# Attention block in fp32r and fp16: two of the four fp32 copies of the attention output are made by POOL instead of ScalarE

## The chip, the cores and the metric

The kernel runs on one core of one Trainium2 chip. The metric is the device time of one execution in microseconds (us); the time of a kernel is the median over its runs. Five engines work side by side and are kept in step by semaphores: PE (TensorE: matmuls, with PEld for its weight loads), DVE (VectorE), ACT (ScalarE), POOL (GpSimd) and SP (SyncE, which here only issues DMAs). Each engine runs its own instructions in the order in which they were written.

## The reference

A group norm with 32 groups over x (4 batches, 512 channels, 48 x 48 = 2304 tokens) is followed by self attention with 8 heads of 64 channels and by an output projection, and x is added:

```
hn  = group_norm(x) * scale + bias
qkv = (qkv_w @ hn + qkv_b)  as fp16           # (b, 3, 8 heads, 64, 2304)
w   = softmax((q*s)^T (k*s))                  # s = 64 ** -0.25
a   = (w @ v)  as fp32                        # (b, 512, 2304)
out = x + proj_w @ a + proj_b
```

## The kernel before

The work is cut into four batches, four pairs of heads in each batch (a pair is 128 channels, so it fills the partitions; g counts the 16 pairs, g = 4b + pair), and for each pair five blocks of queries: four of 512 tokens and a last one of 256 (`QBLOCKS`, j = 0 to 4).

The main loop walks over `stream`, a list of units. A unit is one sixth of a 512-block (one third of a 256-block): three bursts, each with two or four score matmuls on PE (L949) into one of three PSUM tiles `ps`, and one exponential on ACT (L956) from that tile to a fp16 tile `p`. Two units later PE multiplies those exponentials with v (L974). DVE adds up the exponentials for the softmax sums (L1003, tile `acc`; both inputs are in SBUF), at the end of a block with two further adds (L1006).

When a block of a pair is complete, DVE copies the product from PSUM (L983, `avx`), PE sums `acc` over the partitions (L1026), DVE copies the sums (L1042), and DMAs on SP's queue bring them to a small tile and, inverted, back as rows (`sums`, `row`, `ib`). POOL then checks the sums (L1064 and L1065, four small instructions per block, in `check_sums`) and makes `att`, the fp16 attention output: `att = avx * ib` (L1090, in `divide`). POOL also computes `rstd` of the group norm (L631). That is nearly all of what POOL does in the main loop.

The output projection of batch b runs beside the attention of the first pair of batch b+1 (for the last batch, in the last pair and the tail). For each block j, `att32` copies the block of `att` of all four pairs to fp32 tiles `a` (tags `a32_0` to `a32_3`, one buffer each), with ACT at L832. `proj_chain` then runs over the pairs c = 0 to 3 and multiplies each copy with a high and a low part of the weights (L838, eight matmuls in one PSUM bank for one chunk of 128 output channels); there are four chunks per block. DVE adds the bias and the residual (L865) and frees the one bank `pw`, and SP stores the result.

Because the tiles `a` have one buffer, the copies of block j+1 wait until PE has read those of block j for the last time, which is in the last chunk of block j: pair c = 2 is read for the last time by its sixth matmul, pair c = 3 by its eighth.

Where each piece of work goes is decided when the program is written out: `beside` is a hand-ordered list of the pieces of projections, `put_convert` puts the copies of a block (through `begin` in `proj_pieces`) between the chunks of block j and those of block j+1, and `fill` takes pieces from the list after each unit as a credit in microseconds allows. In ACT's order the copies of a block therefore stand between two units' exponentials, in POOL's order between the checks and divisions of whatever blocks are under way.

In the last batch the blocks j = 2, 3, 4 are handled in two parts: `FIRST` (pairs 0 to 2, three copies) and `LAST` (pair 3 alone, one copy). Of the 80 copies, 16 have 256 columns and 64 have 512.

Of the kernel before, what the change touches and what calls it, by code (L numbers as in the profile page):

```python
# [27 lines left out]
NC = C // P  # L28
NPAIR = HEADS // 2
# [438 lines left out]
def fast_path(  # L468
# [12 lines left out]
    nc = tc.nc  # L481
# [303 lines left out]
    atts, res, at32 = {}, {}, {}  # L785
# [32 lines left out]
    def left_over(b, j):  # L818

        return b == B - 1 and j >= NQ - 2  # L820

    def att32(b, j, pairs=range(NC)):
        o, n = QBLOCKS[j]
        for c in pairs:
            if left_over(b, j):
                t = xpool.tile([P, n], F32R, tag=f"x{c}_{j}", name=f"a32_{b}_{j}_{c}")
            else:
                t = work.tile(
                    [P, QB], F32R, tag=f"a32_{c}", bufs=1, name=f"a32_{b}_{j}_{c}"
                )  # L830
            at32[b, j, c] = t[:, :n]
            nc.scalar.copy(at32[b, j, c], atts[b * NPAIR + c][:, o : o + n])  # L832

    def proj_chain(b, j, m, ps, pairs=range(NC)):
        n = QBLOCKS[j][1]
# [52 lines left out]
    def proj_pieces(b, j):  # L888

        def ahead(k):
            if k < len(proj_list) and not in_two(b, proj_list[k][0]):
                residual(b, *proj_list[k])

        def begin():
            att32(b, j, LAST if in_two(b, j) else range(NC))
            if j == 0:
                ahead(0)
                ahead(1)  # L900

        pairs = LAST if in_two(b, j) else range(NC)
        chains = [
            proj_piece(b, j, chunks, pairs, lambda k=k: ahead(k + 2))
            for k, (jj, chunks) in enumerate(proj_list)
            if jj == j
        ]
        return [piece(0.0, begin)], chains
# [271 lines left out]
    for b in range(B):  # L1180
# [20 lines left out]
        if b == B - 1:  # L1201
            put_qk(g + 3, 1)
            put_qk(g + 3, 0, range(NQ - 1))
            put_convert(old, 0)
            put_qk(g + 3, 0, (NQ - 1,))

            ahead = [
                (residual, b, j, chunks)
                for j in (NQ - 2, NQ - 3, NQ - 1)
                for jj, chunks in proj_list  # L1210
                if jj == j
            ]
            for j in range(NQ):
                put_proj(old, j, ahead)
                if j + 1 < NQ:
                    put_convert(old, j + 1)

            for j in (NQ - 2, NQ - 3, NQ - 1):
                there = ends[(NG - 2) * NQ + j] + BEHIND + 6
                put_run(att32, b, j, FIRST, after=there)  # L1220
                put_first(b, j)
            put_convert(b, 0)
            put_proj(b, 0)
            put_convert(b, 1)
            put_proj(b, 1)
            put_convert(b, NQ - 3)
            put_proj(b, NQ - 3)
            continue
# [120 lines left out]
    for n in range(end):  # L1349
# [25 lines left out]
        if n - BEHIND in soon:  # L1375
            g, j = stream[n - BEHIND][:2]
# [9 lines left out]
    g, b, j = NG - 1, B - 1, NQ - 1  # L1386
    n = QBLOCKS[j][1]
    values(stream[-2])
    while loads:
        loads.popleft()[1]()  # L1390
    check_sums(g, NQ - 2)
    att32(b, NQ - 2, LAST)

    def last_banks(name):
# [21 lines left out]
    o = QBLOCKS[j][0]  # L1416
# [39 lines left out]
@with_exitstack  # L1456
def group_norm_attention(ctx: ExitStack, tc: tile.TileContext, *args):
    nc = tc.nc
    keep = ctx.enter_context(tc.tile_pool(name="keep", bufs=1))
    flag = keep.tile([1, 1], I32, name="flag")  # L1460

    kinds = mybir.EngineType
    engines = {kinds.PE, kinds.DVE, kinds.Pool, kinds.SP, kinds.Activation}
    with tc.manual_schedule(engines=engines):
        fast_path(tc, flag, *args)
    fails = nc.values_load(
        flag[0:1, 0:1],
        min_val=0,
        max_val=1,
        skip_runtime_bounds_check_because="it is the result of a comparison",  # L1470
    )
    with tc.If(fails > 0, label="fallback"):
        general_path(tc, *args)
# [37 lines left out]
```

## Time and profile before

| what | value |
|---|---|
| median of 3 runs | 1616.85 us (1616.51 to 1617.53) |
| profiled execution, its own time | 1617.42 us |
| its span (first to last instruction) | 1615.6 us |
| granted TensorE clock | 0.998 |
| ACT copies L832 | 80, 40.7 us, mean 596 ns |
| POOL multiplications L1090 | 78, 117.7 us, mean 1508 ns |
| DVE adds L1003 | 270 of 1796 ns and 79 of 1748 ns (means) |
| ACT idle, waiting for PE's scores | 298.4 us |
| PE idle, waiting for ACT's exponentials | 5.3 us in 12 waits |

The first lines of the page give each engine's busy time, its share of the span and its number of instructions. The groups of instructions give, for one line of the kernel, the engine, what it writes and reads, how often, its busy time and the mean of one. The list of waits says which engine sat idle until which other engine or DMA had finished: total, number, longest. In the timeline a row has the start, the duration, the engine, the line and, in square brackets, the idle time just before it with what ended it.

### The profile page before, as it was taken

How to read it: one execution, taken by the hardware profiler on the slowest of the kernel's cores; microseconds unless marked ns; L12 is line 12 of the kernel's file. 1: busy time of each engine (PE TensorE's matmuls, PEld its weight loads, DVE VectorE, ACT ScalarE, POOL GpSimd, SP SyncE). 2: the span in 40 equal slices, each digit the busy share in tenths (PEclk: the TensorE clock that was granted, in tenths of full speed). 3: DMA queues.
4: the chain of work that ended last, by engine and by line, in shares of the span. 5: the costliest groups of instructions: out<-in, count | busy, mean ns of one | idle time of the engine just before them, and what ended most of it. 6: DMA issues, size and time to landing. Idle time of an engine off the chain costs nothing. (4 is left out here: it accounts for less than half of the span.)

```text
span 1615.6 us, 28324 instructions
## 1 busy us (share of the span) xinstructions
PE 1583.1 (98%) x11500; PEld 695.5 (43%) x11500; DVE 1135.7 (70%) x1301; ACT 1283.0 (79%) x1398; POOL 293.8 (18%) x421
## 2 busy tenths in 40 slices
PE   7999999999999999999999999999999999999996
PEld 2533434443333534555333353455533334434544
DVE  6267668866666668986666666898667666667775
ACT  3077777888888888888887888887888888888894
POOL 1001112212121211212111121121211121211212
PEclk9999999999999999999999999999999999999999
DMA  7002020000000023511000002352100000016424
GB/s 217 6 14 67 11 66 22 18 14 11 14 18 14 13 65 119 158 50 28 14 11 18 14 12 60 98 162 72 31 14 12 14 18 15 15 24 188 123 61 132
DMA packets 94897, 82.11 MB, mean 51 GB/s; under 512 B 50852, under 2 KB 60964, under 8 KB 94756
## 3 DMA queue, kind: packets, MB, share of 16 engines
q1 hardware_dynamic: 92724, 78.35, 17.8%
q8 instruction: 92, 1.51, 0.4%
q10 hardware_dynamic: 1904, 1.84, 0.4%
q14 instruction: 49, 0.40, 0.1%
q0 software_dynamic: 128, 0.01, 0.0%
HBM read 60.70 MB, written 19.17 MB: 49 GB/s over the span
## 5 line engine op out<-in xcount | busy, mean ns | idle before, releaser
L956 ACT ACTIVATE p<-ps 128x1024 f16<-128x1024 f32 x1296 | 1231.9, 1027 | 298.9 <-PE ps L949 298.4
L1003 DVE TENSOR_TENSOR acc<-acc,p 128x3072 f16<-128x3072 f16 x270 | 485.0, 1796 | 77.0 <-ACT p L956 76.2
L709 PE MATMUL pqk<-x,wqkv 128*64 128x512 f32 (+1 forms) x2464 | 519.3, 551 | 0.0
L949 PE MATMUL ps<-q,k 64*128 64x512 f16 (+1 forms) x2880 | 359.5, 358 | 6.3 <-ACT p L956 5.3
L974 PE MATMUL av<-p,v 128*64 128x512 f16 (+1 forms) x2880 | 361.1, 364 | 0.4 <-DVE slx L1042 0.3
L760 PE MATMUL pv<-wqkv,x 128*64 128x256 f32 x2304 | 268.6, 380 | 0.0
L709 PEld LDWEIGHTS pqk<-x,wqkv 128*64 128x64 f32 x2464 | 168.9, 137 | 224.2 <-issue 166.8
L1064 POOL TENSOR_SCALAR in<-sums 128x8 f32<-128x8 f32 (+1 forms) x158 | 112.5, 712 | 782.3 <-DMA sums<-slx 775.9
L949 PEld LDWEIGHTS <-k 64*128 64x128 f16 x2880 | 107.4, 94 | 286.1 <-issue 238.3
L974 PEld LDWEIGHTS <-v 128*64 128x64 f16 x2880 | 131.9, 109 | 211.3 <-issue 167.1
L1090 POOL TENSOR_TENSOR att<-avx,ib 128x512 f16<-128x512 f32 (+1 forms) x78 | 117.7, 1508 | 468.7 <-DMA ib<-row 398.5
L760 PEld LDWEIGHTS pv<-wqkv,x 128*64 128x64 f32 x2304 | 160.1, 137 | 92.8 <-issue 4.5
L1003 DVE TENSOR_TENSOR acc<-p,p 128x3072 f16<-128x3072 f16 x79 | 138.1, 1748 | 0.0
L838 PE MATMUL pr<-a,whi 128*128 128x512 f32 (+1 forms) x311 | 121.8, 399 | 1.7 <-DVE q L719 1.1
L838 PE MATMUL pr<-a,wlo 128*128 128x512 f32 (+1 forms) x311 | 113.5, 372 | 0.0
L1006 DVE TENSOR_TENSOR acc<-acc 128x1024 f16<-128x1024 f16 x156 | 109.2, 700 | 5.3
L719 DVE TENSOR_SCALAR q<-pqk,bqkv 128x512 f16<-128x512 f32 (+1 forms) x79 | 54.9, 695 | 80.3 <-PE pqk L709 79.8
L719 DVE TENSOR_SCALAR k<-pqk,bqkv 128x512 f16<-128x512 f32 (+1 forms) x75 | 52.1, 695 | 77.9 <-PE pqk L709 77.8
L768 DVE TENSOR_TENSOR v<-pv,bv 128x512 f16<-128x512 f32 x72 | 49.7, 691 | 80.5 <-PE pv L760 80.2
L983 DVE COPY avx<-av 128x512 f32<-128x512 f32 (+1 forms) x79 | 50.6, 640 | 66.1 <-PE av L974 66.1
L865 DVE SCALAR_TENSOR_TENSOR r<-pr,bproj,r 128x512 f32<-128x512 f32 (+1 forms) x80 | 54.9, 694 | 43.2 <-PE pr L838 42.6
L838 PEld LDWEIGHTS pr<-a,whi 128*128 128x128 f32 x311 | 58.4, 188 | 38.6 <-issue 18.5
(68 smaller groups left out, 451.0 us busy)
## 6 DMA issues: line engine op xcount, KB each, us to landing
r<-x_dram SPq DMA_DIRECT2D x72, 256.0 KB, 3.2
out_dram<-r SPq DMA_DIRECT2D x69, 256.0 KB, 2.1
ib<-row SPq DMA_DIRECT2D x126, 128.0 KB, 3.1
x<-x_dram SPq DMA_DIRECT2D x62, 256.0 KB, 4.2
x<-x_dram SPq DMA_DIRECT2D x16, 128.0 KB, 4.9
sums<-slx SPq DMA_DIRECT2D x128, 2.0 KB, 2.1
ib<-row SPq DMA_DIRECT2D x30, 64.0 KB, 3.2
wqkv<-qkv_wT_dram SPq DMA_DIRECT2D x2, 768.0 KB, 6.9
```

Source lines behind the costliest of these rows:

```text
L709: nc.tensor.matmul(pw[0][lo : lo + D, :n], wqkv[:, c, w0 + lo : w0 + lo + D], hn[b, c, j], start=(c == 0), stop=(c == NC - 1),)
L719: nc.vector.tensor_scalar(qk[g][part][:, o : o + n], pw[0][:, :n], bqkv[:, col : col + 1], SCALE, ALU.add, ALU.mult,)
L760: nc.tensor.matmul(pw[0][lo : lo + D, a, :], hn[b, c, i * P // QB][:, at + lo : at + lo + D], wqkv[:, c, 2 * C + half * C // 2 :][:, : C / ...
L838: nc.tensor.matmul(ps[:, :n], w[:, c, bass.ts(m, P)], at32[b, j, c], start=(i == 0), stop=(i == len(steps) - 1),)
L865: nc.vector.scalar_tensor_tensor(xt[:, i], places[i], bias, xt[:, i], ALU.add, ALU.add)
L949: nc.tensor.matmul(ps[:, h, a * n : (a + 1) * n], kt[rows, bass.ts(i, P)], qt[rows, o : o + n], start=True, stop=True,)
L956: nc.scalar.activation(pt[:, r], ps, AF.Exp)
L974: nc.tensor.matmul(av[0][lo : lo + D, :n], vv[b, pr // 2][:, i, pr % 2 * P + lo : pr % 2 * P + lo + D], pt[:, r, h, a * n : (a + 1) * n], ...
L1003: nc.vector.tensor_tensor(t, before, pt, ALU.add)
L1006: nc.vector.tensor_tensor(t[:, 0], t[:, 0], t[:, r], ALU.add)
L1064: nc.gpsimd.tensor_scalar(t, sm, limit, None, op)
L1090: nc.gpsimd.tensor_tensor(atts[g][:, o : o + n], avx.pop((g, j))[:, :n], ibs.pop((g, j))[:, :n], ALU.mult,)
```

## The change

`att32` makes the copies of the third and fourth pair (c = 2 and 3) with POOL instead of ACT, wherever it is called for more than one pair. The calls for one pair (`LAST`) are as before, and so are the buffers, PE's, DVE's and SP's instructions and their order.

```
+    beside_exps = range(NC // 2, NC)
+
     def att32(b, j, pairs=range(NC)):
...
             at32[b, j, c] = t[:, :n]
-            nc.scalar.copy(at32[b, j, c], atts[b * NPAIR + c][:, o : o + n])
+            source = atts[b * NPAIR + c][:, o : o + n]
+            if c in beside_exps and len(pairs) > 1:
+                nc.gpsimd.tensor_copy(at32[b, j, c], source)
+            else:
+                nc.scalar.copy(at32[b, j, c], source)
```

## The prediction

> **What bounds the kernel now.** I read the page's first line, then the list of waits, then PE's timeline around every cast at L832. The first line says that PE is the bound:
>
> ```profile
> PE 1583.1 (98%) x11500; PEld 695.5 (43%) x11500; DVE 1135.7 (70%) x1301; ACT 1283.0 (79%) x1398; POOL 293.8 (18%) x421
> ```
>
> PE is idle for 32.5 us of the span, mostly at both ends. So ACT's time is worth nothing in itself; it counts only where its lateness reaches PE. The waits say how often:
>
> ```profile
> ACT p L956 <- PE ps L949: 298.4, 391, 46.7
> ...
> PE ps L949 <- ACT p L956: 5.3, 12, 0.5
> ```
>
> ACT waits 298.4 us for PE, PE only 5.3 us for ACT. But those 5.3 us sit where the change works. Of PE's 12 waits for exponentials, ten follow a block's casts by 4 to 5 us: at 630.22 (0.52), 667.19 (0.39), 1038.46 and 1039.37 (0.16 + 0.52), 1077.14 (0.38), 1092.37 (0.39), 1456.16 (0.52), 1492.54 (0.38), 1542.85 (0.52), 1563.55 us (0.52). Sum: 4.30 us. There are stalls too short for a row of their own: six score matmuls take 0.82 us in 351 of PE's groups, but 0.95 to 1.13 us in seven groups after the other casts (651.38, 681.43, 1061.61, 1507.14, 1528.79, 1555.24, 1578.22). The excess over 0.82 is 1.36 us. The casts cost PE **5.66 us** in all.
>
> [...] POOL's small L1065 has a median of 205 ns and a maximum of 1804, about L1003's 1750; L1003 itself reaches 2851 beside an L1090. Whoever waits gets in after the one running operation: at 1030.14 and 1030.93 us POOL's checks run 0.70 and 0.60 us, one DVE add each.
> [...] I therefore use starts and what waits for them.
>
> **What is moved.** Fifteen blocks of batches 0 to 2 and two of batch 3 move two casts each, three blocks of batch 3 one each: 37, of which 7 have 256 columns. None issues a DMA; PE's, DVE's and SP's orders stay. Durations:
>
> ```profile
> L1090 POOL TENSOR_TENSOR att<-avx,ib 128x512 f16<-128x512 f32 (+1 forms) x78 | 117.7, 1508 | 468.7 <-DMA ib<-row 398.5 <-DVE acc L1003 47.6 <-ACT p L956 11.4
> ...
> L832 ACT CAST a<-att 128x512 fp32r<-128x512 f16 (+1 forms) x80 | 40.7, 596 | 2.7 <-POOL att L1053 2.3 <-PE pr L838 0.5
> ...
> L1430 POOL TENSOR_SCALAR fines<-inv 128x256 f32<-128x256 f32 x1 | 0.9, 853 | 0.1
> ...
> L1434 POOL COPY fines<-fine 128x8 f32<-128x8 f32 x1 | 0.2, 187 | 0.0
> ```
>
> *ACT.* Four casts take 2.19 us, so a further one costs (2.19 - 0.64)/3 = 0.52 us (0.31 with 256 columns). ACT loses 30 x 0.52 + 7 x 0.31 = 17.8 us, 1.04 us per full block. Each stall above is 0.13 to 0.68 us, and no more than what its block gives up. So all **5.66 us** can go, except the 0.68 at 1038 to 1039 us: there the first projection waits 1.10 us for DVE at 1044.88, and DVE for a sums DMA at 1043.09, which a faster ACT does not bring earlier. **Gain 4.98 us.**
>
> *One POOL copy, d.* The trace has none of this size. Below: the 187 ns of the 8-column copy plus 504 columns at the 0.84 ns of POOL's memsets (128x96 217 ns, 128x8 143) is 0.61 us. Above: at the 2.51 ns per column of POOL's tensor_scalar (256 columns 853 ns, 8 columns 231) it is 1.45 us. [...] I take **0.85 us**[...].
>
> *When the copies can start, and when they are needed.* A copy waits for the last read of the old tile. In blocks 1 to 4 that is in the last chunk of the block before, at about the moment ACT's casts start now. PE's next chain begins 1.4 to 2 us later and reads pair 2 1.03 us and pair 3 1.49 us after that. So POOL has 2.5 to 3.4 us for 2 x 0.85 = 1.70 us, if it is free and has the port. In six blocks the release is long past or other chains come first, and nothing can be late: block 0 of each batch, and block 4 of batches 0 and 1. The three `FIRST` copies go early too. I went through the rest with POOL's and DVE's timelines. Blocks 1 of all batches, block 2 of batch 0 and blocks 3 and 4 of batch 2 fit, with DVE adds pushed by up to 0.7 us into idle time. Four do not:
>
> (1) Batch 1, block 2. POOL has L1090 and L631 ahead of the copies, and then DVE holds the port:
>
> ```profile
> 1070.89 1.77 POOL L1090 TENSOR_TENSOR att<-avx,ib 128x512 f16<-128x512 f32 x1 [5.91 <-DMA ib<-row]
> ...
> 1072.15 2.19 ACT L832 CAST a<-att 128x512 fp32r<-128x512 f16 x4
> ...
> 1072.77 0.72 POOL L631 TENSOR_TENSOR rstd<-veps,mhalf 128x2 f32<-128x2 f32 x1
> ...
> 1073.35 1.74 DVE L1003 TENSOR_TENSOR acc<-acc,p 128x3072 f16<-128x3072 f16 x1
> ...
> 1075.12 0.40 PE L838 MATMUL pr<-a,whi 128*128 128x512 f32 x1
> 1075.13 1.42 DVE L1006 TENSOR_TENSOR acc<-acc 128x1024 f16<-128x1024 f16 x2
> ...
> 1077.14 0.39 PE L949 MATMUL ps<-q,k 64*128 64x512 f16 x2 [0.38 <-ACT p L956]
> ```
>
> The first copy can be issued at 1073.55, behind L1003's start, gets the port at 1075.1 and is ready at 1076.05[...]; the row at 1075.12 wants it: 0.93 late. The second waits for the first L1006 (to 1076.55), is ready at 1077.5 and wanted at 1076.51: 1.0. **1.9 us.**
>
> (2) Batch 2, block 2. L1090 stands ahead and waits for its DMA:
>
> ```profile
> 1487.55 2.19 ACT L832 CAST a<-att 128x512 fp32r<-128x512 f16 x4
> ...
> 1488.06 1.28 POOL L1090 TENSOR_TENSOR att<-avx,ib 128x512 f16<-128x512 f32 x1 [7.79 <-DMA ib<-row]
> ...
> 1488.74 2.21 DVE L1003 TENSOR_TENSOR acc<-acc,p 128x3072 f16<-128x3072 f16 x1
> ...
> 1490.53 0.39 PE L838 MATMUL pr<-a,whi 128*128 128x512 f32 x1
> ```
>
> Issued at 1489.4, behind an L1003 that L1090 has held up (2.21 us), the first copy gets the port at 1490.95, is ready at 1491.9 and wanted at 1490.53: 1.37. The second, behind an L1006, loses 1.04. **2.4 us.**
>
> (3) Batch 0, block 3. The first copy is released between the two L1006 of 676.56 us and goes first; the second L1006 then ends at 678.7 instead of 677.98, the L865 behind it, which frees the only bank `pw`, at 679.45 instead of 678.63, and the chain of 679.02 starts **0.83 us** late. Here it is DVE's queue that is hit.
>
> (4) Batch 1, block 3. The checks end at 1087.71, the first copy at 1088.65; the second finds L1003 (from 1088.57) on the port until 1090.35, is ready at 1091.3 and wanted at 1090.82: **0.48 us.**
>
> *What is queued behind the copies on POOL:* checks, divisions and one `rstd`. A division is needed many units later, and two `avx` and `rows` buffers cover a delay of 2 to 3 us. The `rstd` of batch 0 (666.34 us) may come 2 us later, against its reader at 668.84: 0 to 0.5 us of DVE, ahead of an L865 at 670.44, so nothing.
>
> **Sum.** Losses 1.9 + 2.4 + 0.83 + 0.48 = 5.6 us, gain 4.98: **+0.6 us**. The profiled execution took 1617.42 us with a span of 1615.6, so it would take 1618.0; it lies 0.6 above the median of 1616.85, which becomes 1617.5.
>
> **The rivals.** What a measurement of this kernel can tell from no change is about 0.2%, 3.2 us.
>
> *Balance* (the forecast): the gain is real and POOL's late copies give it back.
>
> *All copies are in time, faster.* For it: POOL is 18% busy, and most blocks leave it a microsecond. Against: (1) and (2) come from POOL's order, which is fixed. With d = 0.61 the four losses fall by 0.24 for each copy on the path (once in (3), twice in (1) and (2)) and (4) goes: 5.6 - 0.48 - 5 x 0.24 = 3.9, net -1.1. Only if POOL also wins the port in (1), (2) and (3) is it the whole -5.0: 1611.9 us.
>
> *The copy is slow, slower.* At the price of tensor_scalar, d = 1.45, two copies take 2.9 us, as long as the time from release to need. (1) and (2) then lose 1.2 us more each, (3) and (4) 0.6 each, and blocks 1 of batches 0 and 1 begin to be late by 0.15: 9.5 - 5.0 = +4.5 us, 1621.4. It decides from about d = 1.3, where the losses exceed the gain by 3.2 us. For it: the trace's only wide one-input POOL operation costs 2.51 ns per column, and each longer copy holds up DVE's adds for longer, with bank releases behind them. Against: a copy computes nothing.
>
> *Nothing changes* is excluded: the built program has 37 more instructions on POOL and 37 fewer on ACT.
>
> **Chances.** Balance 0.5; in time 0.2; slow copy, or bank releases held up in more places than (3), 0.3. Balance alone spans 1615 to 1620; the range of 8 in 10 takes in part of both sides: 1612.5 to 1622.5. Faster by over 0.2% (below 1613.6) 0.19, within 0.49, slower (above 1620.1) 0.32.
>
> **What would show it.** In the changed profile, a POOL copy of 512 columns near 0.85 us where alone; ACT about 18 us less busy; PE's waits for exponentials from 5.3 down to about 1.7 us (0.68 or less at 1038, 1.03 at 1465 to 1466, where no cast is near); and new PE or PEld waits for POOL's `a` of 1 to 2.4 us near 1075 and 1491 us, and for L865 near 679. If those waits are absent, the port argument is wrong; if they appear in more than five blocks, d is.

## The result and the profile after

The changed kernel takes 1614.47 us (median of 22 runs, 1612.90 to 1617.04); the kernel before took 1616.88 us in the 22 runs beside it (1615.97 to 1618.40). The ratio is 0.9985, 95% interval 0.9979 to 0.9992: the change saves **2.4 us**. Forecast was +0.6 us. The time lies in the stated range and the saving is below 0.2%, but the sign of the sum was wrong. The profiled execution after took 1614.36 us with a span of 1612.6 us.

The page's first line after, in the same columns as before:

```profile
PE 1583.4 (98%) x11500; PEld 695.7 (43%) x11500; DVE 1140.2 (71%) x1301; ACT 1268.4 (79%) x1361; POOL 319.4 (20%) x458
```

PE's busy time is what it was (1583.1 before). ACT is 14.6 us less busy (its exponentials take 2.3 us more), POOL 25.6 us more. The copies in the groups of instructions, now with two lines:

```profile
L836 POOL CAST a<-att 128x512 fp32r<-128x512 f16 (+1 forms) x37 | 24.9, 692 | 59.4 <-PE pr L844 51.9 <-PE pqk L709 7.3
L838 ACT CAST a<-att 128x512 fp32r<-128x512 f16 (+1 forms) x43 | 23.0, 591 | 2.7 <-POOL att L1059 2.3 <-PE pr L844 0.5
```

ACT's copies went from 40.7 to 23.0 us: 17.7 us, where 17.8 were worked out. POOL's mean of 692 ns includes copies that ran beside DVE's adds (the longest took 2.14 us); two copies undisturbed take 1.18 us (at 645.97 and at 660.24 us), so d, the time of one POOL copy, is 0.59 us, not 0.85. "The port" (in two expectations "the shared port") is here a name for what the traces show and no more: a POOL instruction and a DVE add that meet hold each other up. In the kernel before, POOL's L1065 of 1028.47 us ended at 1030.07, 0.05 us after the L1003 of 1028.27, and took 1.60 us where its median is 0.205; in the changed kernel the two L1012 of 1074.67 us take 2.00 us beside POOL's copies, where the two L1006 of the kernel before (1075.13) took 1.42. By what means they do so, no run shows. And PE's list of waits:

```profile
PE pr L844 <- DVE q L719: 2.3, 1, 2.3
...
PE pr L844 <- POOL a L836: 1.7, 4, 0.8
PE ps L955 <- ACT p L962: 1.4, 3, 0.5
```

The waits for exponentials fell from 5.3 to 1.4 us. Four waits for POOL's copies came in, 1.7 us. The single wait for DVE's `q`, 1.10 us before, is 2.3 us now. That is no more than a first view: the experiments show that these rows give the places rightly and the sizes wrongly.

The first late place, in the changed kernel's timeline:

```profile
1072.31 0.72 POOL L631 TENSOR_TENSOR rstd<-veps,mhalf 128x2 f32<-128x2 f32 x1
...
1072.89 1.74 DVE L1009 TENSOR_TENSOR acc<-acc,p 128x3072 f16<-128x3072 f16 x1
1072.99 3.14 POOL L836 CAST a<-att 128x512 fp32r<-128x512 f16 x2
...
1073.63 0.50 PE L844 MATMUL pr<-a,whi 128*128 128x512 f32 x1
...
1074.67 2.00 DVE L1012 TENSOR_TENSOR acc<-acc 128x1024 f16<-128x1024 f16 x2
...
1075.16 0.50 PE L844 MATMUL pr<-a,whi 128*128 128x512 f32 x1 [0.34 <-POOL a L836]
...
1076.18 0.50 PE L844 MATMUL pr<-a,whi 128*128 128x512 f32 x1 [0.28 <-POOL a L836]
...
1076.84 0.33 PEld L955 LDWEIGHTS <-k 64*128 64x128 f16 x6 [0.36 <-issue]
```

This is the forecast order: `rstd` ahead on POOL, DVE's L1009 until 1074.63, the first copy after it (its matmul starts at 1075.16), a DVE add, and the second copy (it ends at 1076.13, and its matmul starts at 1076.18; the recorded ready times allow 0.1 us where this shows 0.05). Two copies that need 1.18 us alone span 3.14. The chain from its first matmul to the next scores takes 76.84 - 73.63 = 3.21 us, where the kernel before took 2.06 (1074.09 to 1076.15):

```profile
1074.09 0.50 PE L838 MATMUL pr<-a,whi 128*128 128x512 f32 x1
...
1076.15 0.60 PE L949 MATMUL ps<-q,k 64*128 64x512 f16 x4
```

So 1.15 us are lost, while the two rows show 0.34 + 0.28 = 0.62. The second place, around 1489 us, has the same picture: rows of 0.81 and 0.29, a chain of 3.69 against 2.05 us.

The place that the forecast had settled with a deduction of 0.68 us:

```profile
1034.54 1.80 SPq L512 DMA_DIRECT2D x<-x_dram  x4
...
1036.43 1.15 SPq L1051 DMA_DIRECT2D sums<-slx  x2
...
1041.33 0.18 DVE L1077 RECIPROCAL inv<-sums 128x4 f32<-128x4 f32 x1 [2.90 <-DMA sums<-slx]
...
1042.59 0.47 DVE L719 TENSOR_SCALAR q<-pqk,bqkv 128x256 f16<-128x256 f32 x1
...
1043.12 0.50 PE L844 MATMUL pr<-a,whi 128*128 128x512 f32 x1 [2.34 <-DVE q L719]
```

On SP's queue four loads of x (for block 3 of batch 3) stand ahead of the two small sums DMAs, and DVE's reciprocal, which waits for their landing, starts 4.9 us after the first was issued (the medians of these DMAs from issue to landing are 2.1 us for the 128 of 2.0 KB and 2.2 us for the 30 of 1.0 KB); `q` stands behind the reciprocal on DVE, and PE is idle 2.34 us ahead of its first projection matmul. The same place in the kernel before:

```profile
1038.42 1.15 SPq L1045 DMA_DIRECT2D sums<-slx  x2
...
1043.09 0.18 DVE L1071 RECIPROCAL inv<-sums 128x4 f32<-128x4 f32 x1 [1.98 <-DMA sums<-slx]
...
1044.88 0.50 PE L838 MATMUL pr<-a,whi 128*128 128x512 f32 x1 [1.10 <-DVE q L719]
```

What follows in the changed kernel is in the table of windows (length, busy time of PE, PEld, DVE, ACT and POOL, then the granted TensorE clock, the DMA share and GB/s):

```profile
1043.70:1047.00 3.30, 3.30 (x11) 1.89 (x11) 1.58 (x2) 0.01 (x1) 0.00 (x0) 0.50 0.27 33
```

In this stretch of 3.3 us after the wait the clock is 0.50. In the kernel before, after its wait of 1.10 us, it was 1.00 at the same work (1044.80 to 1047.00 us). The projection matmuls start 0.43 us apart here (1044.07 to 1044.50), 0.23 us apart there (1045.69 to 1045.92).

### The profile page after: what moved, and what is told of

Read it like the earlier page. It is cut to its first block, busy times and chain, and to the rows that moved or that the text cites. A ratio compares the mean times of both kernels' runs of the same rounds, so it can differ in the third digit from the quotient of the medians.

```text
span 1612.6 us, 28321 instructions
## 1 busy us (share of the span) xinstructions
PE 1583.4 (98%) x11500; PEld 695.7 (43%) x11500; DVE 1140.2 (71%) x1301; ACT 1268.4 (79%) x1361; POOL 319.4 (20%) x458
## 3 DMA queue, kind: packets, MB, share of 16 engines
q1 hardware_dynamic: 92724, 78.35, 17.8%
q8 instruction: 92, 1.51, 0.4%
## 5 line engine op out<-in xcount | busy, mean ns | idle before, releaser
L1009 DVE TENSOR_TENSOR acc<-acc,p 128x3072 f16<-128x3072 f16 x270 | 488.3, 1809 | 69.8 <-ACT p L962 69.1
L1070 POOL TENSOR_SCALAR in<-sums 128x8 f32<-128x8 f32 (+1 forms) x158 | 118.4, 749 | 713.3 <-DMA sums<-slx 706.8
L1096 POOL TENSOR_TENSOR att<-avx,ib 128x512 f16<-128x512 f32 (+1 forms) x78 | 117.2, 1502 | 451.1 <-DMA ib<-row 424.8
L1009 DVE TENSOR_TENSOR acc<-p,p 128x3072 f16<-128x3072 f16 x79 | 138.2, 1749 | 0.0
L1012 DVE TENSOR_TENSOR acc<-acc 128x1024 f16<-128x1024 f16 x156 | 111.8, 716 | 5.4
L989 DVE COPY avx<-av 128x512 f32<-128x512 f32 (+1 forms) x79 | 50.6, 641 | 63.7 <-PE av L980 63.6
L871 DVE SCALAR_TENSOR_TENSOR r<-pr,bproj,r 128x512 f32<-128x512 f32 (+1 forms) x80 | 54.9, 695 | 45.2 <-PE pr L844 44.7
```

The costliest lines, as they stand in the source:

```text
L871: nc.vector.scalar_tensor_tensor(xt[:, i], places[i], bias, xt[:, i], ALU.add, ALU.add)
L1009: nc.vector.tensor_tensor(t, before, pt, ALU.add)
L1012: nc.vector.tensor_tensor(t[:, 0], t[:, 0], t[:, r], ALU.add)
L1070: nc.gpsimd.tensor_scalar(t, sm, limit, None, op)
L1096: nc.gpsimd.tensor_tensor(atts[g][:, o : o + n], avx.pop((g, j))[:, :n], ibs.pop((g, j))[:, :n], ALU.mult,)
```

## The experiments

All ratios are to the kernel before, with 95% intervals. To place a loss I also use the starts of DVE's `avx` copy (L983 before, L989 after): there is one for each block of a pair but the very last, 79 in all, and the start before minus the start in another kernel is that kernel's lead at this block. The leads are those of one profiled execution each.

**1. Without POOL's copies.** From the second block on nobody copies the pairs 2 and 3, except in the `LAST` calls.

```
+            if c in beside_exps and len(pairs) > 1 and c in kept:
+                at32[b, j, c] = kept[c][:, :n]
+                continue
```

> ACT makes the copies of pairs 0 and 1 only, as in the changed kernel; POOL makes the two copies of the first block of batch 0 and none after it, and PE reads those two old tiles in every later block (so pairs 2 and 3 of the later projections are computed from old data). This is the gain without POOL's cost. Theory A (of the 5.3 us that ACT gives back, 1.7 us are lost to late POOL copies in two blocks, and about 2.8 us in batch 1, block 0, where PE waits for DVE and a sums DMA that a faster ACT does not bring earlier): 1.7 us below the changed kernel, that is -4.1 us against before, and the wait of about 2.3 us near 1043 us stays. Rival B (POOL's copies hold DVE up on the shared port, and that wait is theirs): the wait falls back to 1.1 us or less, and the kernel is 5.5 to 7 us faster than before.

Measured 1610.48 us against 1616.53, ratio 0.9966 (0.9952 to 0.9979): -6.05 us. No PE wait for POOL is left, but the wait for `q` is still 2.4 us. So POOL's copies are not the cause of that wait; a faster ACT is enough. The saving is as large as rival B expected, but not for its reason, since the wait stayed: ACT's shorter copies gain more than the idle rows say, as shown below.

**2. Each POOL copy made twice.**

```
                 nc.gpsimd.tensor_copy(at32[b, j, c], source)
+                nc.gpsimd.tensor_copy(at32[b, j, c], source)
```

> Every POOL copy is issued twice, so the pair takes about 2.3 us instead of 1.18. Theory A: PE waits for POOL only where POOL's order or the port makes a copy late; the two late blocks lose another 1.2 us each and few others join: about +2.4 us against the changed kernel, 0 against before. The sum on record (losses of 5.6 us at 0.85 us a copy, 0.6 us more for each 0.1 us) gives +2.5 us against before. Rival B (the port): twice the hold-ups on DVE everywhere, +4 us or more against before, with new PE waits for DVE's bank releases in most blocks.

Measured 1627.09 us, ratio 1.0067 (1.0053 to 1.0081): +10.6 us. That is on rival B's side (+4 or more), but not with its waits for bank releases in most blocks: PE waited 9.6 us in ten places for POOL and 2.3 us in four for L872. In the profiled execution at least 2.7 us of it are the clock's, as an estimate from its mean of 0.73 over 1494 to 1504 us (0.27 x 10). Twice the copies are twice the work, but also twice as many instructions that can meet a DVE add: in the change, at 1072.99 us, two copies of 0.59 us each took 3.14 us beside DVE's adds. This test mixes the two.

**3. The change, with the loads of x one unit later.** The loads that stood ahead of the sums DMA are issued after it.

```
-        loads.append((now[0] + 1, run))
+        loads.append((now[0] + (2 if (b, j) == (3, 3) else 1), run))
```

> The changed kernel, with one group of four loads (x of batch 3, block 3, 256 KB each) issued one unit later, so that on SP's queue it stands behind the sums DMAs of the block under way and not ahead of them. Theory A: DVE's wait for those sums near 1041 us goes, PE's wait of 2.34 us goes, and with it the eight projection matmuls that ran at 0.43 us apart instead of 0.23: -2.8 us against the changed kernel, -5.2 against before. Rival B (DVE is late for another reason): no more than -0.5 us against the changed kernel, and the wait stays. Rival C (the loads only move the wait to the next transfer): a wait of DVE or PE for another DMA appears within 15 us, and the sum is the same.

Measured 1609.19 us (1608.00 to 1610.67), ratio 0.9958 (0.9944 to 0.9971): **-7.3 us**, the lowest time of a kernel that leaves nothing out; it beats the kernels before and after. SP's queue in its timeline:

```profile
1033.47 1.14 SPq L1051 DMA_DIRECT2D sums<-slx  x2
1034.71 1.96 SPq L512 DMA_DIRECT2D x<-x_dram  x4
```

The sums are ahead, the wait for `q` is gone, and PE has no gap from 1036 to 1044 us. Of PE's waits for POOL only 0.67 and 0.28 us near 1484 are left; the copies near 1075 are in time too. One changed line of issue order thus gave 4.9 us on top of the change. By the `avx` starts 3.95 of it come from the wait for `q` and what followed it, and 0.97 from the copies near 1075, which the edit does not touch: the work of the other engines falls otherwise there.

**4. The kernel before, with the same later loads.**

> The kernel before with the same four loads one unit later. Theory A: PE's wait of 1.10 us near 1044.9 goes, and the 0.68 us of waits for exponentials before it stay: -1.1 us against before. If the later loads were worth as much without the change as with it (rival D: the change and the loads have nothing to do with each other), -2.8 us.

Measured 1615.07 us (13 runs), ratio 0.9991 (0.9982 to 0.9999): -1.5 us, near theory A; in the `avx` starts the lead it gains at this place is 1.15. The order of the loads was worth 1.15 us before the change and, as shown below, 3.95 after it.

**5. A longer copy, made of two.**

```
                 nc.gpsimd.tensor_copy(at32[b, j, c], source)
+                nc.gpsimd.tensor_copy(at32[b, j, c][:, :128], source[:, :128])
```

> The changed kernel; behind each POOL copy a second one of its first 128 columns is issued (about 0.25 us at 0.19 us plus 0.8 ns per column), so that a copy takes about the 0.85 us of the prediction instead of the 0.58 measured. Theory A (the prediction's step that failed is this duration): each late copy costs 0.27 us more, twice in each of the two late blocks, and some further blocks begin to be late: +1.8 to +3.5 us against the changed kernel, within 1.5 us of before. Rival (the duration did not decide; the gain was underestimated): +0.5 us or less.

Measured 1621.31 us, ratio 1.0032 (1.0020 to 1.0044): +5.2 us, more than either expectation. A copy and its supplement take 0.91 us undisturbed, so this was to be the forecast's d. It was no clean test: the extra instruction takes 0.30 us alone but up to 1.89 us (the copy itself 0.61 at the median and up to 2.14), so each of the two can be held up, by DVE's adds if they behave as the copies at 1072.99 us in the change; and in the profiled execution 1.7 us are a fall of the clock, as an estimate from its mean of 0.79 over 1076 to 1084 us (0.21 x 8). What it suggests is that the number of POOL instructions counts beside their length. Test 9 repeats it with one instruction.

**6. POOL's divisions behind the copies.** `divide` is called after `fill`, except for the last pair.

```
-        if block_at(n - BEHIND - 4):
-            divide(*block_at(n - BEHIND - 4))
+        over = block_at(n - BEHIND - 4)
+        if over and over[0] == NG - 1:
+            divide(*over)
...
+        if over and over[0] < NG - 1:
+            divide(*over)
```

> The changed kernel with POOL's divisions (all but the last pair's) written out behind the pieces of the projection of the same unit instead of ahead of them. Only POOL's order changes: in batch 2, block 2 the copies stand ahead of the division that waits for its DMA, in batch 1, block 2 they stand behind the rstd and ahead of the division. Theory A (late copies are a matter of POOL's order): batch 2, block 2 loses nothing (its chain takes 2.05 us again instead of 3.69), batch 1, block 2 keeps most of its loss: -1.6 us against the changed kernel. Rival (the port decides; DVE's add comes first in any order): no change.

Measured 1612.78 us (14 runs), ratio 0.9977 (0.9969 to 0.9985): -3.3 us. Of the waits for POOL 0.3 us remain, and in batch 2, block 2 the chain takes 2.06 us again (1487.03 to 1489.09): there the lateness came from what stood ahead on POOL. Blocks 50 to 54, where place (1) lies, gain no more than in the change (-0.17 us against +0.01). And PE now waits 1.4 us for L871, which frees the bank `pw`, where it waited 0.3. Its interval overlaps the change's; the step from -2.4 to -3.3 is not shown to be real.

**7. Later loads and later divisions together.**

> The changed kernel with both edits: the four loads one unit later and the divisions behind the projection's pieces. Theory A: the two add up, as far as a late copy is left: with the loads later alone only batch 2, block 2 still waits for POOL (0.67 + 0.28 us), so another -1.5 us: -8.5 to -9 us against before, the fastest version here, with no wait of PE for POOL. Rival: the gains do not add, -7.3 as with the later loads alone.

Measured 1609.37 us, ratio 0.9956 (0.9942 to 0.9969): the same as with later loads alone; the expected further 1.5 us did not come. No wait of PE for POOL is left, and 1.4 us of waits for L871 have taken its place.

**8. Later loads, and only the fourth pair on POOL.**

```
-    beside_exps = range(NC // 2, NC)
+    beside_exps = range(NC - 1, NC)
```

> As with the later loads, but only the copy of pair 3 is made by POOL; ACT makes three. Theory A: ACT gives back 0.52 us per block instead of 1.04, which is about what each wait for exponentials was, and POOL's one copy is late only in batch 2, block 2, by some 0.3 us less than two: within 1 us of the later loads with two pairs. If ACT's lateness is larger than its rows of 0.52 us show[...], half the copies leave part of the waits in place: 1.5 to 3 us slower than with two pairs.

Measured 1611.82 us (9 runs), ratio 0.9975 (0.9965 to 0.9985): -4.3 us, 2.4 us less saved than test 7, run beside it with both pairs on POOL (the two intervals overlap a little, but the slowest run of test 7 took 1609.61 us and the fastest here 1611.30). That is what was expected if ACT's lateness is larger than its rows show. PE's waits for exponentials are 2.5 us against 1.4, and one of 0.5 us at a projection. The second pair is worth its POOL time.

**9. The same copies as one longer instruction.**

```
-                nc.gpsimd.tensor_copy(at32[b, j, c], source)
+                nc.gpsimd.tensor_scalar(at32[b, j, c], source, 1.0, None, ALU.mult)
```

> POOL makes the same two copies of every block, one instruction each as in the change, but as tensor_scalar (times 1.0) instead of a copy, which takes it longer: its duration d is the quantity that the record staked 0.6 us of the total per 0.1 us on. Theory A (the copies' size was the wrong term, and the record's slope is right): if d comes out near 1.45 us, +4.5 us against the kernel before (about 1621), waits for POOL's copy of some 5 to 6 us in the sum and more blocks than the two late ones; if d comes out near 0.85, +0.6. Theory B (a longer copy also pushes DVE's operations back at the shared port and the lateness compounds): +8 to +12 us at 1.45. Rival C (d hardly matters since the cost sits elsewhere): within 1 us of the change, -2.4 us.

Measured 1624.21 us (1619.81 to 1626.02), ratio 1.0050 (1.0036 to 1.0064): +7.65 us, between the expected +4.5 and +8 to +12. The answer for this line (minimum, median and maximum in ns):

```profile
L836 POOL TENSOR_SCALAR a<-att x37: 842/1492/2879, 623.9 to 1577.8; 128x512 fp32r<-128x512 f16 x30, 128x256 fp32r<-128x256 f16 x7
```

So d is 1.49 us, the record's upper bound, but for the operation that it was taken from, not for a copy. (From the record's own two points, 853 ns for 256 columns and 2.51 ns for each further one, it is 1.50; the 1.45 starts from the 187 ns of the small copy.) PE's rows of waits for POOL sum to 4.9 us in five places. The late place at 1075 us:

```profile
1073.52 0.50 PE L844 MATMUL pr<-a,whi 128*128 128x512 f32 x1
...
1075.94 0.50 PE L844 MATMUL pr<-a,whi 128*128 128x512 f32 x1 [1.22 <-POOL a L836]
...
1077.67 0.79 PE L844 MATMUL pr<-a,whi 128*128 128x512 f32 x1 [1.00 <-POOL a L836]
...
1078.82 1.46 PE L955 MATMUL ps<-q,k 64*128 64x512 f16 x6
```

The chain takes 78.82 - 73.52 = 5.30 us, 3.24 more than before; the record had 1.9 + 1.2 = 3.1 for this case. The scores after it take 1.46 instead of 0.82 us, with a clock of 0.80 over 1074 to 1080 us. The fall lies inside the chain: from 1077.67 us its last starts are 0.59 and 0.56 us apart (0.34 and 0.32 in the change, from 1076.18), so some 0.5 of the 3.24 us are the clock's.

**10. The ceiling: no POOL copies and later loads.** The edits of tests 1 and 3 together. (The expectation places the loads at the end of batch 0; they are those of block 3 of batch 3, issued beside the first projection pieces of batch 1.)

> Left out: the two copies of pair 2 and 3 from the second block on (the projection reads the tiles of the first block), so that nothing waits for them; and the reload of x at the end of batch 0 is issued one unit later, which takes the late division of the next batch's first block away. It is the ceiling of the change. Theory A (each idle row of PE understates its stall, gross gain about 7.9 us): -9 us against the kernel before, 7.9 of it from ACT's copies and 1.15 from the division. Rival B (the rows are right at 5.66 us): -6.8 us. Either way no wait of PE at the projections remains above 0.4 us, and the kernel with the copies and the later reload (-7.3) lies 1.7 us above it under A and within 1 us of it or below under B.

Measured 1607.68 us against 1616.56, ratio 0.9946 (0.9932 to 0.9959): -8.9 us, where the larger gross gain was to give -9 and the rows at face value -6.8. The interval (-11.0 to -6.6 us) just holds the other value too, so its `avx` starts carry the point, in the next section.

## Why the sum came out wrong

The leads at the `avx` starts, in us gained in each stretch of blocks (profiled executions, blocks counted from 0; ahead of block 27, before the first copy, the kernels' leads already differ by up to 1.0 us; that is left out):

| blocks (work of the projection in them) | ceiling (10) | the change | longer copy (9) |
|---|---|---|---|
| 27 to 49 (batch 0) | +1.94 | +1.51 | -0.12 |
| 49 to 50 (first block of batch 1) | +2.20 | -1.75 | -0.06 |
| 50 to 54 (rest of batch 1) | +1.12 | +0.01 | -4.36 |
| 54 to 71 (none) | +0.02 | -0.01 | -0.01 |
| 71 to 78 (batch 2, batch 3) | +3.83 | +2.37 | +0.94 |
| sum | +9.11 | +2.13 | -3.61 |

Nothing changes where no projection runs: the whole effect lies at the projections, as forecast. The columns' differences give the three terms of the recorded sum:

| term | record | measured | how |
|---|---|---|---|
| gain of ACT's shorter casts | -5.66 | -7.96 | 9.11 less the 1.15 of test 4 |
| what the transfer at 1043 us takes back | +0.68 | +2.80 | 2.20 + 1.75 = 3.95, less the 1.15 that it cost before |
| late copies | +5.6 | +3.0 | 0.43 + 1.11 + 1.46 in the other rows |
| sum | +0.6 | -2.2 | the change's own sum: -2.13; median of the runs: -2.4 |

The errors of the first two terms, 2.3 and 2.1 us, nearly cancel. That is luck, since most of the second is a fall of the clock. So the sign turned on the third: the late copies cost 2.6 us less than forecast.

**The gain was mis-sized: idle rows were taken at face value.** The same work in PE's timeline, before the change:

```profile
628.81 0.89 PE L949 MATMUL ps<-q,k 64*128 64x512 f16 x4
630.22 0.39 PE L949 MATMUL ps<-q,k 64*128 64x512 f16 x2 [0.52 <-ACT p L956]
630.55 0.84 PE L974 MATMUL av<-p,v 128*64 128x512 f16 x6
631.22 1.89 PE L709 MATMUL pqk<-x,wqkv 128*64 128x256 f32 x16
```

and after it:

```profile
628.33 0.82 PE L955 MATMUL ps<-q,k 64*128 64x512 f16 x6
629.09 0.84 PE L980 MATMUL av<-p,v 128*64 128x512 f16 x6
629.76 1.89 PE L709 MATMUL pqk<-x,wqkv 128*64 128x256 f32 x16
```

From the first score to the q and k matmuls it was 2.41 us and is 1.43: 0.98 saved where the row said 0.52. The rest stood inside "busy" time: four matmuls 0.89 us, where six take 0.82. Starts against starts thus give another size than the gaps, and the same holds for the waits for POOL (0.62 in rows, 1.15 in starts). The prediction used starts for POOL and not for PE.

**The 0.68 us were the wrong size, and the clock was missed.** The deduction was right in kind: what PE gains between the issue of the sums DMA and the matmul that needs `q` is lost again. The transfer itself moves with PE. Before and after the change its first DMA is issued 5.55 and 5.54 us after the start of block 49's `avx` copy (1032.87 and 1030.89 us), and DVE's reciprocal starts 4.67 and 4.90 us after the issue. But PE comes to its wait 10.91 us after that start before the change and 9.89 us after it, as the stalls of 1038 to 1039 us are gone: 1.02 us where their rows said 0.68. With the 0.23 us that the transfer took longer the wait grew from 1.10 to 2.34 us.

And the clock fell after it: from 1043.50 to 1047.50 us the granted clock was 0.57, which as an estimate is 0.43 x 4 = 1.7 us, for which the sum had no term. (By starts, from the first projection matmul after the wait to the first of the next chain, it is 5.11 us, 1043.12 to 1048.23, against 3.58 before, 1044.88 to 1048.46: 1.53.) The longer wait and the clock are 1.24 + 1.7 = 2.9 us, or 2.8 by starts; 2.80 were measured. Test 9, with a wait of 2.18 us and the clock at 1.00 after it, lost 2.20 + 0.06 = 2.26 here: the wait alone. What was gained in batch 0 is not lost at this place: test 2 was 1.5 us behind the kernel before at block 49 and waited 2.1 us all the same. Test 3 took the cause away.

**The copies were late by half of what was forecast: d was the wrong term.** The lower bound of the record (0.61 us, from the 8-column copy and the memsets) was nearly right, and the value taken, 0.85, was the author's own estimate between the two bounds, shown by no trace; the cast takes 0.59 us. (By their records the copies of 256 and of 512 columns take 0.39 and 0.61 us: 0.86 ns per column, about the 0.84 of the memsets.) At d = 0.59, 0.26 less for each copy, the record's own four losses are 1.9 - 0.52 = 1.38, 2.4 - 0.52 = 1.88, 0.83 - 0.26 = 0.57 and 0: 3.8 us. Places (1) and (2) came about as described, with 1.11 and (in blocks 71 to 74) 1.43 us by the `avx` starts. Places (3) and (4) did not: the copies began at 675.33 us (the pair in 1.63) and at 1087.80 us (in 1.18, ahead of the L1009 of 1088.69, which takes 1.89 instead of 1.75 us), and PE waited at neither. Instead 0.32 us of waiting for L871 came at 644.25 us, behind an L1009 of 2.56 us (from 639.52 us; 2.23 before) that an L1096 held up (639.19 to 640.46 us), with no copy near: some 0.3 of the 0.43 us in the first row of the table, which are no late copy's.

**What was right:** that PE bounds the kernel and ACT's 17.7 us are worth only what reaches PE; the two places where POOL's order and DVE's adds make the copies late, and the port, in the sense given above, as the reason; that the two stalls without a cast near stay (0.51 and 0.53 us at 1464.10 and 1465.01; beside them 0.34 of 0.52 us are left at 1541.51). The slope in d held in the one traced execution of test 9: it lost 10.4 us in the rows of the table other than the second (ceiling less test 9: 2.06 + 5.48 + 2.89), 1.7 of it through the clock, where the record's losses at d = 1.45 are 9.5. But that was the fastest of five runs, 4.4 us below their median. The other four (1623.5 to 1626.0 us) had mean granted clocks of 0.994 to 0.996 against 0.998; as an estimate, a thousandth of the clock is 1.6 us of a PE-bound span of 1618.1 us, so the clock can account for most of the difference. Without their traces that is not shown.

The rival "all in time" erred on the same term: it expected a net of -1.1 us at d = 0.61. That -2.4 came near it is partly luck, since the gain was 2.3 us larger and the take-back 2.1 us larger than in that sum.

**What stays open:** why the clock falls after one wait and not after another (below); whether later divisions help the change without later loads (test 6); and what a longer copy of the same form would cost, since test 5 adds instructions and test 9 changes the operation.

## What to carry to other kernels

Size a stall on PE by starts, from the last undisturbed matmul to the next group, against the same work elsewhere without the stall; the idle time in the row showed little more than half of it at 630 us, and the record's whole sum, 5.66, was 0.71 of the 7.96 gained. Before pricing a faster engine, find the transfers whose landing it doesn't hasten, here a small DMA behind four large ones on one queue: what is gained between the issue of such a transfer and its use is lost at it (here 1.02 us), and the longer wait can cost the clock too (here 1.7 us, estimated from the clock). A change of issue order worth 1.15 us alone was worth 3.95 at the same place once ACT was faster, 1.7 of it by that estimate the clock's. Work moved to POOL cost by its duration (test 9: +7.65 us against the change's -2.4) and, as tests 2 and 5 suggest, by its number of instructions: two copies of 0.59 us each took 3.14 us where both met DVE's adds.

## What the runs showed of the hardware that was not expected

- **The granted clock fell after some waits of about 2 us of PE and not after others; a fall is 1.7 us, as an estimate from the clock.** Just after a wait for `q` it was 0.50 after 2.34 us (the change), and it fell too after 2.4 (test 1) and 1.73 (test 6), but was 1.00 after 2.5 (test 5), 2.18 (test 9) and 2.1 (test 2). The mean is 0.57 over 4.0 us in the change (1043.50 to 1047.50) and in test 1 (1044 to 1048), and 0.59 over 4.2 us in test 6 (1041.80 to 1046.00). It fell, too, around two waits close together, 1.22 and 1.00 us (test 9: 0.80 over 1074 to 1080 us, 0.87 over 1080 to 1084). What decides between a fall and none is not shown. The mean of the granted clocks is 0.9965 over the change's 22 runs and 0.998 over the runs with later loads (tests 3 and 7) and of the kernel before. That the falls widen the spread of the times (4.1 us over the change's runs, 2.4 over those beside them) is likely, not shown.
- **POOL cast 512 columns of fp16 to fp32 in 0.59 us** (the change), but took 1.49 us (median of test 9's records) for the same columns as a multiplication by 1.0. The form of the instruction was worth about 10 us of this kernel's time: 1624.21 us, +7.65, against -2.4.
- **A small second POOL instruction is not always small:** 128 columns took 0.30 us alone (test 5, 1057.59 us) and up to 1.89 us; that a DVE add held up the longest is likely from the copies at 1072.99 us of the change, not shown.
